# A masked attention layer on one core: scores moved, an eighth home for Q and K, row statistics moved, another set of resident weight sums

## The chip, the cores and the metric

The kernel runs on one core of one Trainium2 chip. The metric is the device time of one execution in microseconds. The core has TensorE (PE, with its weight loads PEld), VectorE (DVE), ScalarE (ACT), GpSimd (POOL) and SyncE (SP), which issues nearly all DMA transfers here.

## What is computed

```python
def layer(x, adj, Wq, bq, Wk, bk, Wv, bv, beta):      # x (128, 128, 768), adj (128, 128, 128), 12 heads of 64
    h = jnp.maximum(_layernorm(x, axis=-1), 0.0)
    q = _split_heads(h @ Wq + bq)
    k = _split_heads(h @ Wk + bk)
    v = _split_heads(h @ Wv + bv)
    scores = jnp.einsum('bhqd,bhkd->bhqk', q, k) / jnp.sqrt(HD)
    adj_e = adj[:, None, :, :]
    scores = jnp.where(adj_e > 0, scores + beta * adj_e, -9000000000000000.0)
    probs = jax.nn.softmax(scores, axis=-1)
    out = jnp.einsum('bhqk,bhkd->bhqd', probs, v)
    return x + out.transpose(0, 2, 1, 3).reshape(B, N, D)
```

All data is float32.

## The kernel before

**Groups and slices.** The 128 batches are worked off in 32 groups of four (`G` from 0 to 31). For each group three products with weights are made, called slices: `qk0` (Q and K of the first six heads), `v` (V of all heads) and `qk1` (Q and K of the last six heads). Group 0 uses plain matrix products (`plain_slice`). In groups 1 to 31 each slice is 15 block products (`product_z`, L525) of a fast matrix multiplication: an activation operand (a block of the transposed normalized rows, `A..`, or a sum of such blocks, `S..`) times a sum of weight blocks (`T`). Each product is 28 matmuls in the profile (L541) and adds to one of four chains a, b, c, d, each of which holds a pair of PSUM banks. The pairs are four in all; score stages and attention take one from the same four.

**Order.** In groups 1 and later nothing is left to a scheduler (`manual_schedule`): `run` (L775) emits a product's matmuls, then the steps listed for its number (`todo`, by `then`), then the masks of scores made before (`masking`), then decodes that are due (`overdue`), then the product's evictions, the trailing ScalarE work, and last the steps listed as "post". Every engine works its instructions off in that order. `ORDER` gives the products' order in a slice. Below, "product n" is the n-th in that order, from 0.

**Weight sums.** The 45 sums T are made once and kept in DRAM, but for those whose places (0 to 44 over the three slices) stand in `RESIDENT` (L114), which stay in SBUF. The others are streamed in every group, 448 KB each, through a ring of five buffers (`load_T`, L325, DMA at L330): when a streamed product has been emitted, the load of the streamed sum five further on is issued on SP's queue.

**Homes and decodes.** A product's result is added out of PSUM into a home, a block of SBUF for one of the six outputs (r, j) of a slice (`home_qk`; additions at L565, first evictions at L555, L556, L559, L561). When an output has all its products, it is decoded on GpSimd (`decode`, L573; L581 to L584 for Q and K, L592 to L596 for V, which goes on into `vring` and frees the home). Homes of Q and K are freed when their scores are emitted. There are six homes, and a seventh in the area `sbig` from group 0's last slice on.

**Scores and attention.** `scores(G, u, j)` (L609, matmuls at L618) needs the two outputs (0, j) and (1, j) of slice `qk`u; it takes a pair, and in the next product VectorE masks and biases it (L626), gives the pair back, and ScalarE takes the exponential (L628). `attend` (matmuls at L671) follows in later products, threaded between their matmuls; `load_xo` (L605) fetches its residual rows. The scores of `qk0` are taken in the `v` slice of the same group. The scores of `qk1` (u = 1) are taken in the `qk0` slice of the next group, at products 1, 3 and after 5.

**Preparation of later groups.** For group G + 2, the rows' mean and variance come from eight half rows (`load_half`, DMA at L404, into three buffers in turn; `half_stats` on VectorE, L412 and L414), in the `v` slice; `row_moments` (L416) turns them into scale and shift (VectorE L420 and L422, GpSimd L424 and L425), which go to DRAM and back by two small transfers (L428, L429) a few products later. `norm` (L439, ScalarE) applies them to x, loaded by `load_x` in four pieces (L189); `to_hT` (L450, VectorE) transposes, and `inner` (L460 to L462, GpSimd) adds the block sums within an `A`. `sum_acts` (L455, VectorE) makes the sums `S..`.

Of the kernel before, what the change touches and what calls it, by code (L numbers as in the profile page):

```python
# [10 lines left out]
F32 = mybir.dt.float32  # L11
# [6 lines left out]
P = 128  # L18
# [12 lines left out]
@with_exitstack  # L31
def kernel(
    ctx: ExitStack,
    tc: tile.TileContext,
    x: bass.AP,
    adj: bass.AP,
    wq: bass.AP,
    bq: bass.AP,
    wk: bass.AP,
    bk: bass.AP,  # L40
    wv: bass.AP,
    bv: bass.AP,
    beta: bass.AP,
    out: bass.AP,
):

    nc = tc.nc
    keep = ctx.enter_context(tc.tile_pool(name="keep", bufs=1))
    bad = keep.tile([1, 1], I32, name="bad")
    args = (x, adj, wq, bq, wk, bk, wv, bv, beta, out)
    direct(tc, *args, bad)
    again = nc.values_load(bad[0:1, 0:1])
    with tc.If(again > 0):
        general(tc, *args)
# [51 lines left out]
LORDER = (1, 4, 0, 8, 5, 2, 10, 3, 6, 7, 13, 9, 11, 12, 14)  # L111
ORDER = {"qk0": ZORDER, "v": ZORDER, "qk1": QORDER}
RING = 5
RESIDENT = (3, 7, 10, 14, 18, 22, 25, 29, 33, 37, 40, 44)  # L114


SPOT = ("S7", "S0", "S5", "S14", "S11", "S6", "S1", "S9", "S10", "S2")
# [8 lines left out]
def direct(ctx, tc, x, adj, wq, bq, wk, bk, wv, bv, beta, out, bad):  # L126
# [14 lines left out]
    NG = B // GRP  # L141
# [10 lines left out]
    const = ctx.enter_context(tc.tile_pool(name="const", bufs=1))  # L152
# [107 lines left out]
    sequence = [(sl, n) for sl in ("qk0", "v", "qk1") for n in ORDER[sl]]  # L260
    resident = {key: const.tile([P, 7, P], F32, name=f"res_{key[0]}_{key[1]}") for key in (sequence[at] for at in RESIDENT)}
    kept, tz = {}, {}
# [55 lines left out]
    def order_of(G, sl):  # L318
        return LORDER if G == NG - 1 and sl == "qk1" else ORDER[sl]
# [184 lines left out]
        while between and next(between[0], None) is None:  # L504
            between.popleft()

    homes = deque(const.tile([P, 7, P], F32, name=f"home{i}") for i in range(6))
    home_of = {}

    def home_qk(G, sl, r, j, zones=False):  # L510
# [264 lines left out]
    def run(products, todo):  # L775
        for at, steps in enumerate(products):
            next(steps)
            behind_product(at, todo)
            next(steps)
            trail()  # L780
            for f in todo.get((at, "post"), ()):
                f()

    def slice_z(G, sl, todo):
        run([product_z(G, sl, n) for n in order_of(G, sl)], todo)
# [163 lines left out]
    def then(at, f, *args):  # L949
        todo.setdefault(at, []).append(lambda: f(*args))  # L950

    def bias(G, *at):
        def go():
            if G not in steps:
                steps[G] = bias_steps(G)
            next(steps[G], None)
        for n in at:
            then(n, go)

    def attention(G, u, at):  # L960
        for n, j in at:
            then(n - 3, load_xo, G, 3 * u + j)
            then((n, "post"), attend, G, 3 * u + j, 5)
# [6 lines left out]
    def turn_act(G, slots):  # L970
        for at, name in slots:
            then(at, to_hT, G, int(name[1]), int(name[2]))
            then(at, inner, G, name)

    def sums_at(G, slots):
        for at, name in slots:
            then(at, sum_acts, G, name)
# [35 lines left out]
    todo.clear()  # L1013
    for n, j in ((1, 0), (2, 1), (3, 2)):
        then((n, "post"), scores, 0, 0, j)
    attention(0, 0, ((11, 2), (13, 1), (15, 0)))
    for n in range(14):
        then(n, step, 2)
    then(1, halve_bias)
    turn_act(1, ((3, "A01"), (4, "A02"), (5, "A00"), (9, "A10"), (10, "A11"), (11, "A12")))  # L1020
    sums_at(1, ((12, "S1"), (13, "S9"), (14, "S10"), (15, "S2")))
    then(12, homes.append, block(len(SPOT)))
    bias(1, 4, 5, 6, 7)
# [4 lines left out]
    for G in range(1, NG):  # L1028
        more = G + 1 < NG
        todo.clear()  # L1030
        then(1, scores, G - 1, 1, 2)
        then(3, scores, G - 1, 1, 0)
        then((5, "post"), scores, G - 1, 1, 1)
        attention(G - 1, 1, ((7, 2), (10, 0), (12, 1)))
        if G == 1:
            sums_at(1, ((0, "S6"), (1, "S7"), (2, "S0"), (5, "S5"), (7, "S14"), (9, "S11")))
            then((0, "post"), load_x, 2, 0)
            for n, at in enumerate((0, 0, 0, 3, 4, 5, 6, 7)):
                then((at, "post"), load_half, 2, n)
            for n, at in enumerate((3, 4, 5, 6, 7, 8, 9, 10)):  # L1040
                then(at, half_stats, 2, n)
            then(10, row_moments, 2, 3, 5)
        else:
            sums_at(G, ((0, "S7"), (1, "S0"), (4, "S5"), (7, "S14"), (9, "S11")))
            if more:
                for g in range(2):
                    for h in range(2):
                        then((2 * g + h, "post"), norm, G + 1, g, 2 * h, 2 * h + 2)
                turn_act(G + 1, ((5, "A01"), (6, "A00"), (11, "A02")))
                then((12, "post"), load_x, G + 1, 1)  # L1050
        slice_z(G, "qk0", todo)

        todo.clear()
        then(0, scores, G, 0, 2)
        then(2, scores, G, 0, 1)
        then(7, scores, G, 0, 0)
        if more:
            then((11, "post"), add_raw, G + 1)
            if G == 1:
                for g in range(2):  # L1060
                    then((2 + g, "post"), norm, 2, g)
                turn_act(2, ((5, "A01"), (6, "A00"), (7, "A02"), (14, "A11")))
                then((8, "post"), load_x, 2, 1)
                for g in range(2, GRP):
                    then((10 + g, "post"), norm, 2, g)
            else:
                for n, at in enumerate((5, 6, 8, 9)):
                    then((at, "post"), norm, G + 1, 2 + n // 2, n % 2 * 2, n % 2 * 2 + 2)
                turn_act(G + 1, ((12, "A11"),))
            if G + 2 < NG:  # L1070
                for n, at in enumerate((0, 0, 0, 3, 5, 6, 8, 9)):
                    then((at, "post"), load_half, G + 2, n)
                for n, at in enumerate((3, 5, 6, 8, 9, 11, 12, 13)):
                    then(at, half_stats, G + 2, n)
        slice_z(G, "v", todo)

        todo.clear()
        if not more:
            break
        attention(G, 0, ((3, 2), (9, 1), (12, 0)))  # L1080
        turn_act(G + 1, ((1, "A10"), (4, "A12")))
        sums_at(G + 1, ((6, "S1"), (7, "S9"), (8, "S2"), (9, "S6"), (10, "S10")))
        bias(G + 1, 0, 2, 4, 5)
        if G + 2 < NG:
            then(5, row_moments, G + 2)
            then((6, "post"), load_x, G + 2, 0)
        slice_z(G, "qk1", todo)

# [150 lines left out]
```

## Time and profile before

| what | value |
|---|---|
| runs | 2904.47, 2900.88, 2901.08 us |
| median | 2901.08 us |
| the profiled execution | 2902.2 us |
| its span, first to last instruction | 2900.4 us |
| mean granted clock of TensorE | 0.97 |
| VectorE, GpSimd, ScalarE busy | 80%, 74%, 52% of the span |
| DMA, main queue | 698.45 MB, 79.2% of 16 engines |

A line of the profile names the source line, the engine, the operation and its tiles (output <- inputs), its shape and how often it stands there; where an engine was idle before it, brackets show for how long and what ended it. Times in the timeline are us from the span's start. One group of the middle runs there from about 1406 (start of `v`) over `qk1` (from 1433) into the next `qk0` (from 1460) and to the next `v` (1495).

### The profile page before, as it was taken

The numbers are of one execution on the slowest core, as the hardware profiler recorded it, in microseconds if no ns is written. First come the engines' busy times: TensorE is split into PE (matmuls) and PEld (weight loads), VectorE is DVE, ScalarE is ACT, GpSimd is POOL, SyncE is SP. The second block draws the span as 40 slices with busy tenths as digits, with TensorE's granted clock in tenths as the row PEclk, the third lists the DMA queues.
The fourth block names the chain that finished last, engine by engine and source line by source line (L and its number), as shares of the span: only waits on it lengthen the run. The fifth ranks groups of instructions, "written<-read, shape, count | busy, mean of one in ns | idle before, by whom it ended". The sixth has DMA issues, their size and how long they took to land.

```text
span 2900.4 us, 121318 instructions
## 1 busy us (share of the span) xinstructions
PE 2753.9 (95%) x52029; PEld 2621.5 (90%) x52029; DVE 2325.4 (80%) x3212; ACT 1497.1 (52%) x3791; POOL 2157.1 (74%) x3170
## 2 busy tenths in 40 slices
PE   9999999999999999999999999999999999999998
PEld 7699998999998989999999999989999999999997
DVE  6897787878888878888878888778887778888775
ACT  1455555555555555555555555555555555555543
POOL 4677777777878777777778787777877787877775
PEclk9999999999999999999999999999999999999999
DMA  8797777978878887788788788787887877888765
GB/s 212 233 282 244 244 229 247 270 246 255 243 233 254 260 249 242 233 253 271 238 249 241 235 256 259 251 237 230 254 271 243 244 242 238 255 259 254 230 212 154
DMA packets 543011, 707.02 MB, mean 244 GB/s; under 512 B 107388, under 2 KB 406152, under 8 KB 542472
## 3 DMA queue, kind: packets, MB, share of 16 engines
q1 hardware_dynamic: 541312, 698.45, 79.2%
q8 instruction: 411, 6.73, 0.9%
q10 hardware_dynamic: 1160, 0.79, 0.1%
q14 instruction: 128, 1.05, 0.1%
HBM read 633.51 MB, written 65.59 MB: 241 GB/s over the span
## 4 chain that ended last, share of the span: by engine, by line
POOL 57%; PE 23%; issue 12%; DVE 4%; ACT 0%; POOLq 0%; DMA 0%; SPq 0%; ACTq 0%; DVEq 0%
PE pair L541 19%; POOL home L584 7%; POOL home L582 6%; POOL home L581 6%; POOL home L583 5%; POOL v L596 5%; POOL home L594 5%; POOL v L595 4%; POOL A L461 3%; POOL home L593 3%; POOL A L460 3%; PE pair L618 3%; POOL v L592 3%; DVE home L565 2%; POOL A L462 2%
## 5 line engine op out<-in xcount | busy, mean ns | idle before, releaser
L565 DVE TENSOR_TENSOR home<-home,pair 128x896 f32<-128x896 f32 x798 | 847.2, 1071 | 235.8 <-PE pair L541 193.4
L541 PE MATMUL pair<-sbig,T_qk 128*64 128x128 f32 x14756 | 961.5, 281 | 7.6 <-DMA T_qk<-kept_qk 4.0
L541 PEld LDWEIGHTS pair<-sbig,T_qk 128*64 128x64 f32 x14756 | 841.4, 142 | 28.3 <-issue 24.5
L654 ACT ACTIVATE e<-e,sm 128x64 f32<-128x64 f32 x1512 | 382.3, 336 | 270.4 <-DVE sm L642 270.3
L541 PE MATMUL pair<-T_v,sbig 128*64 128x128 f32 x7812 | 456.1, 273 | 0.8 <-ACT sbig L556 0.5
L541 PEld LDWEIGHTS pair<-T_v,sbig 128*64 128x64 f32 x7812 | 430.6, 137 | 7.3 <-issue 5.4
L671 PE MATMUL pair<-v,e 128*64 128x65 f32 x6048 | 402.9, 222 | 8.9 <-POOL v L596 8.2
L559 ACT ACTIVATE home<-pair 128x640 f32<-128x640 f32 x319 | 223.5, 700 | 329.5 <-PE pair L541 328.1
L671 PEld LDWEIGHTS pair<-v,e 128*64 128x64 f32 x6048 | 357.8, 137 | 19.9 <-POOL v L596 15.5
L626 DVE SCALAR_TENSOR_TENSOR e<-pair,biasT 128x1024 f32<-128x1024 f32 x189 | 228.0, 1206 | 145.0 <-PE pair L618 141.9
L541 PE MATMUL pair<-A,T_qk 128*64 128x128 f32 x4340 | 333.5, 273 | 0.3 <-DVE home L565 0.2
L460 POOL TENSOR_TENSOR A<-A 128x256 f32<-128x256 f32 x186 | 140.3, 754 | 213.4 <-DVE A L450 213.4
L584 POOL TENSOR_TENSOR home<-home 128x256 f32<-128x256 f32 x319 | 279.5, 876 | 25.0
L618 PE MATMUL pair<-home 64*64 64x128 f32 x5216 | 209.2, 285 | 91.9 <-POOL home L583 85.3
L581 POOL TENSOR_TENSOR home<-home 128x256 f32<-128x256 f32 x319 | 235.6, 739 | 74.0 <-DVE home L565 70.3
L628 ACT ACTIVATE e<-e 128x1024 f32<-128x1024 f32 x189 | 199.9, 1058 | 166.6 <-DVE e L626 166.5
L618 PEld LDWEIGHTS pair<-home 64*64 64x64 f32 x5216 | 144.2, 136 | 141.2 <-POOL home L583 95.0
L541 PE MATMUL pair<-A,res_qk 128*64 128x128 f32 x4340 | 264.3, 273 | 1.0 <-ACT home L561 1.0
L680 ACT COPY e<-pair 128x520 f32<-128x520 f32 x189 | 111.2, 588 | 290.1 <-PE pair L671 289.9
L582 POOL TENSOR_TENSOR home<-home 128x256 f32<-128x256 f32 x319 | 237.0, 743 | 25.0
L541 PEld LDWEIGHTS pair<-A,res_qk 128*64 128x64 f32 x4340 | 240.8, 137 | 1.3 <-ACT home L561 1.3
L439 ACT ACTIVATE x<-x,block 128x192 f32<-128x192 f32 x480 | 234.2, 540 | 3.6 <-DMA x<-in_x_dram 3.6
(186 smaller groups left out, 4656.2 us busy)
## 6 DMA issues: line engine op xcount, KB each, us to landing
T_qk<-kept_qk SPq DMA_DIRECT2D x682, 448.0 KB
T_v<-kept_v SPq DMA_DIRECT2D x341, 448.0 KB
xo<-in_x_dram SPq DMA_DIRECT2D x189, 256.0 KB
out_dram<-xo SPq DMA_DIRECT2D x189, 256.0 KB
x<-in_x_dram SPq DMA_DIRECT2D x248, 192.0 KB
sbig<-in_x_dram SPq DMA_DIRECT2D x186, 192.0 KB
half<-in_x_dram SPq DMA_DIRECT2D x60, 192.0 KB
kept_qk<-prep_qk SPq DMA_DIRECT2D x22, 448.0 KB
```

Of the source, the lines that this page charges most:

```text
L439: nc.scalar.activation(t, t, AF.Relu, bias=shift[G, n], scale=rstd[G, n])
L460: e.tensor_tensor(t[:, 0:2], t[:, 7:8].to_broadcast([P, 2, P]), t[:, 5:7], ALU.subtract)
L541: nc.tensor.matmul(p[q:q + HD, at, :], lhs[:, q:q + HD], rhs, start=(first and at % 4 == 0), stop=True, skip_group_check=True)
L559: nc.scalar.activation(t[:, 0:5], p[:, 0:5], AF.Copy, scale=float(sign))
L565: nc.vector.tensor_tensor(t, t, p[:, 0:7], op)
L581: e.tensor_tensor(t[:, 1:4:2], t[:, 1:4:2], twice(5), ALU.add)
L582: e.tensor_tensor(t[:, 2:5:2], t[:, 2:5:2], twice(1), ALU.add)
L584: e.tensor_tensor(t[:, 0:7:6], t[:, 0:7:6], twice(2), ALU.add)
L618: nc.tensor.matmul(ps[k:k + HD, i, g * N:(g + 1) * N], keys[r, k:k + HD], queries[r], start=True, stop=True)
L626: nc.vector.scalar_tensor_tensor(e, ps, SCORE_CAP * ISCALE, bias, op0=ALU.min, op1=ALU.add)
L654: nc.scalar.activation(o[:, r, b, 0:HD], pa[:, r, b, 0:HD], AF.Copy, scale=t[:, 1, r, b:b + 1])
L671: nc.tensor.matmul(pa[q:q + HD, 2 * g + i, :], k[:, q:q + HD], vt[G, "v", r, h // 4][:, 4 * g + h % 4, :], start=True, stop=True, skip_gro ...
```

## The change

Five places of the schedule change.

- The scores of `qk1` go from products 1, 3 and after 5 of the next `qk0` slice to products 3, 5 and after 6. Group 0's own attention and transpositions of the first slices are shifted by one or two products too.
- There are seven homes to begin with, eight with the one in `sbig`.
- `RESIDENT` has eleven places instead of twelve, nearly all of them others: 34 sums are streamed in each group instead of 33.
- Half rows are loaded from the end of `qk0` on (after products 11, 12 and 13, then after V's products 0 to 4) and their statistics are taken at V's products 0 to 7; `row_moments` goes from `qk1`'s product 5 to V's product 8, and its two small transfers with it.
- The transposition and inner sums of A11 go from V's product 12 to 10.

```diff
-RESIDENT = (3, 7, 10, 14, 18, 22, 25, 29, 33, 37, 40, 44)
+RESIDENT = (3, 8, 12, 16, 20, 25, 29, 33, 35, 38, 41)
...
-    homes = deque(const.tile([P, 7, P], F32, name=f"home{i}") for i in range(6))
+    homes = deque(const.tile([P, 7, P], F32, name=f"home{i}") for i in range(7))
...
-    attention(0, 0, ((11, 2), (13, 1), (15, 0)))
+    attention(0, 0, ((9, 2), (11, 1), (13, 0)))
...
-    turn_act(1, ((3, "A01"), (4, "A02"), (5, "A00"), (9, "A10"), (10, "A11"), (11, "A12")))
+    turn_act(1, ((4, "A01"), (5, "A02"), (6, "A00"), (9, "A10"), (10, "A11"), (11, "A12")))
...
-        then(1, scores, G - 1, 1, 2)
-        then(3, scores, G - 1, 1, 0)
-        then((5, "post"), scores, G - 1, 1, 1)
+        then(3, scores, G - 1, 1, 2)
+        then(5, scores, G - 1, 1, 0)
+        then((6, "post"), scores, G - 1, 1, 1)
...
+        for n, at in enumerate((11, 12, 13) if G + 2 < NG else ()):
+            then((at, "post"), load_half, G + 2, n)
         slice_z(G, "qk0", todo)
...
-                turn_act(G + 1, ((12, "A11"),))
+                turn_act(G + 1, ((10, "A11"),))
             if G + 2 < NG:
-                for n, at in enumerate((0, 0, 0, 3, 5, 6, 8, 9)):
-                    then((at, "post"), load_half, G + 2, n)
-                for n, at in enumerate((3, 5, 6, 8, 9, 11, 12, 13)):
-                    then(at, half_stats, G + 2, n)
+                for n in range(8):
+                    then(n, half_stats, G + 2, n)
+                    if n > 2:
+                        then((n - 3, "post"), load_half, G + 2, n)
+                then(8, row_moments, G + 2)
         slice_z(G, "v", todo)
...
         if G + 2 < NG:
-            then(5, row_moments, G + 2)
             then((6, "post"), load_x, G + 2, 0)
         slice_z(G, "qk1", todo)
```

## What was predicted

> **What bounds the kernel now.** I read the page first, then TensorE's own waits, then one group of four batches on each engine, and last whole groups against each other. The page (columns: busy time, share of the span, instructions):
>
> ```profile
> span 2900.4 us, 121318 instructions
> PE 2753.9 (95%) x52029; PEld 2621.5 (90%) x52029; DVE 2325.4 (80%) x3212; ACT 1497.1 (52%) x3791; POOL 2157.1 (74%) x3170
> ```
>
> TensorE is busy for 95%, so only its gaps and its slow stretches can be won. TensorE's waits (total us, times, longest):
>
> ```profile
> PE pair L618 <- POOL home L583: 85.3, 26, 3.5
> PE pair L618 <- POOL sbig L583: 13.6, 4, 3.4
> PE pair L618 <- POOL home L584: 4.9, 14, 0.4
> PE pair L541 <- DMA T_qk<-kept_qk: 4.0, 1, 4.0
> ```
>
> The first two lines are 30 waits for some 30 groups: one score stage in each group waits up to 3.5 us for the decoding of Q and K on GpSimd. Streamed weight sums (T) made TensorE wait once. Here is that wait in TensorE's timeline, at the start of a QK0 slice:
>
> ```profile
> 1459.57 3.23 PE L541 MATMUL pair<-sbig,T_qk 128*64 128x128 f32 x56
> 1462.73 0.67 PE L618 MATMUL pair<-home 64*64 64x128 f32 x16
> 1466.79 0.45 PE L618 MATMUL pair<-home 64*64 64x128 f32 x8 [3.39 <-POOL home L583]
> 1467.59 0.45 PE L618 MATMUL pair<-home 64*64 64x128 f32 x8 [0.35 <-POOL home L584]
> 1467.97 2.71 PE L541 MATMUL pair<-sbig,T_qk 128*64 128x128 f32 x28
> 1470.46 2.46 PE L541 MATMUL pair<-sbig,res_qk 128*64 128x128 f32 x28
> 1472.85 1.10 PE L618 MATMUL pair<-home 64*64 64x128 f32 x32
> 1473.88 3.28 PE L541 MATMUL pair<-sbig,T_qk 128*64 128x128 f32 x56
> ```
>
> Products 0 and 1 (56 matmuls) take 3.16 us to the next start. A score stage takes 1473.88 - 1472.85 = 1.03 us; this one takes 1467.97 - 1462.73 = 5.24, so 4.21 are lost. And products 2 and 3 then take 1472.85 - 1467.97 = 4.88 instead of some 3.1. The windows (length, busy times of PE, PEld, DVE, ACT, POOL, then clock, DMA share, GB/s) say why, and compare whole groups from score stage to score stage:
>
> ```profile
> 1462.70:1468.00 5.30, 1.55 (x36) 0.87 (x34) 1.43 (x2) 4.04 (x11) 4.99 (x7) 1.00 0.73 210
> 1468.00:1473.00 5.00, 5.00 (x64) 4.83 (x64) 4.21 (x4) 1.93 (x3) 4.61 (x7) 0.66 0.25 66
> 1462.73:1551.03 88.30, 84.24 (x1646) 81.09 (x1644) 72.35 (x97) 47.09 (x121) 67.39 (x99) 0.98 0.82 247
> 2349.80:2438.60 88.80, 85.02 (x1650) 81.57 (x1648) 71.95 (x97) 47.01 (x121) 67.51 (x99) 0.96 0.80 247
> 2616.90:2702.50 85.60, 82.44 (x1649) 79.39 (x1647) 72.81 (x97) 47.54 (x123) 66.67 (x97) 1.00 0.84 253
> ```
>
> After the wait the granted clock is 0.66 for 5 us. The last group kept a clock of 1.00 throughout and lasts 85.60 us rather than 88.3 to 88.8. Its wait was shorter:
>
> ```profile
> 2616.95 0.67 PE L618 MATMUL pair<-home 64*64 64x128 f32 x16
> 2621.30 1.75 PE L541 MATMUL pair<-sbig,T_qk 128*64 128x128 f32 x28
> ```
>
> 4.35 us for the stage, so 3.32 lost; without it that group is 82.28 us. Between the two first starts of this kind (1462.73 and 2616.95) lie 13 groups, 88.8 us each. So the wait with its slow clock costs about 6.5 us in an ordinary group and 3.3 in a rare one; I take 6.1 over 30 groups, for the first groups are shorter: **183 us that can be won**, which would leave 82.3 us a group.
>
> The Trainium skill, page "TensorE: Matmul & The Clock Gate", section Part 1 (the clock gate), says the clock is halved after an idle window of about 3.4 us and that a busy window restores it. The rows agree (3.39 us idle, then 0.66; a shorter idle, then 1.00). Without that rule the sum would be the waits alone, some 104 us less the costs below, which gives 2851 us; with it a shortened wait is worth more than its own length.
>
> **The change part by part.** The stage that waits is the first of the three deferred ones (QK1, pair 2): it needs the fourth of six decodes that GpSimd does one after another. These rows are GpSimd and VectorE in the same group:
>
> ```profile
> 1429.61 0.46 POOL L592 TENSOR_TENSOR v<-home 128x128 f32<-128x128 f32 x1 [3.80 <-DVE home L565]
> 1432.48 0.73 POOL L460 TENSOR_TENSOR A<-A 128x256 f32<-128x256 f32 x1
> 1434.24 0.46 POOL L592 TENSOR_TENSOR v<-home 128x128 f32<-128x128 f32 x1
> 1453.08 1.02 POOL L424 TENSOR_TENSOR row<-verow,nhalf 128x4 f32<-128x4 f32 x1
> 1454.34 0.73 POOL L581 TENSOR_TENSOR home<-home 128x256 f32<-128x256 f32 x1
> 1462.00 1.19 POOL L583 TENSOR_TENSOR home<-home 128x128 f32<-128x128 f32 x1
> 1463.26 1.45 POOL L584 TENSOR_TENSOR home<-home 128x256 f32<-128x256 f32 x1
> 1472.27 1.19 POOL L583 TENSOR_TENSOR sbig<-sbig 128x128 f32<-128x128 f32 x1
> ...
> 1427.44 2.08 DVE L565 TENSOR_TENSOR home<-home,pair 128x896 f32<-128x896 f32 x2 [1.04 <-PE pair L541]
> 1474.02 1.23 DVE L626 SCALAR_TENSOR_TENSOR e<-pair,biasT 128x1024 f32<-128x1024 f32 x1 [0.88 <-PE pair L618]
> 1475.16 0.70 DVE L450 STREAM_TRANSPOSE A<-x 128x512 f32<-128x512 f32 x1
> ```
>
> GpSimd idles until 1429.61 and then shows no gap until the sixth decode ends (1472.27, and one operation more).
>
> *Scores two products later.* The stage moves from product 1 to 3, which is 3.1 us on TensorE: of 4.21 us some 1.1 remain.
>
> *Statistics and A11 earlier.* The inner sums of A11 (1432.48 to 1434.24: 1.76 us) go from V's product 12 to 10, the row moments (1453.08 to 1454.34: 1.26 us) from QK1's product 5 to V's product 8. Both then fall ahead of 1429.61, into GpSimd's idle 3.80 us, and the chain of decodes is shorter by 3.02. VectorE's transposition of A11 (0.70) goes into its idle 1.04 before 1427.44; if the normalizing on ScalarE is late, the eviction behind it and so the chain's start slip by up to 1.3 us (my estimate: one transposition and one short eviction). So the fourth decode comes 1.7 to 3.0 us sooner, against 1.1 needed: **this wait is gone, with 0.6 to 1.9 us to spare**, and with it the slow clock. The second and third stage move by two products and by one: the sixth decode ends at about 1474.2 - 1.7 = 1472.5, and the third stage, undelayed, wants it at about the same time. That is level.
>
> *What is late next: a PSUM pair.* Three chains hold three of the four pairs, so score stages share the fourth. The second and third stage now stand one product apart instead of two and a half. The third can't start before VectorE has masked the second (1.23), behind an eviction (1.04, half of the 2.08) and a transposition (0.70): some 3.0 us after product 5 ends, against 1.03 + 1.5 on TensorE. Cost 0.4 us a group; 0 if the transposition slips behind, 1.5 if the sum for product 4 is late too.
>
> *The eight half rows.* Their loads start three products sooner, and each statistic stands three products behind its load; VectorE takes the eight in V's products 0 to 7 rather than in 3 to 13. If a half is late, VectorE stands still, and behind it wait the masks (which free the pair for the next scores), the evictions, and through them SP's next half load and the T loads in the queue. Rows for it (SP's issues, then VectorE's wait for a half and a mask, then TensorE):
>
> ```profile
> 1408.95 0.99 SPq L404 DMA_DIRECT2D sbig<-in_x_dram  x2
> 1491.36 1.87 SPq L189 DMA_DIRECT2D x<-in_x_dram  x4
> ...
> 1415.41 0.56 DVE L412 BATCH_NORM_STATS2 strow<-sbig 128x6 f32<-128x384 f32 x1 [2.06 <-DMA sbig<-in_x_dram]
> 1497.53 1.23 DVE L626 SCALAR_TENSOR_TENSOR e<-pair,biasT 128x1024 f32<-128x1024 f32 x1
> ...
> 1500.60 1.31 PE L618 MATMUL pair<-home 64*64 64x128 f32 x32
> ```
>
> A half issued at 1408.95 landed at 1415.4: 6.4 us. The second half now stands right behind the four pieces of x, so it is issued at 1493.2 and lands near 1499.6. Its statistic (0.56) stands ahead of the mask that ran at 1497.53; the mask would end at 1501.4, and the scores of 1500.60 wait 0.8 us. Halves 3 to 7 have three products and up to two score stages from issue to need (4.6 + 2.1 us), with the same latency; I put 0.4 on them together. Cost 1.2 us a group; nothing if all land as fast as TensorE allows; above, 3.8 us for one that comes 3.4 late with a slowed clock.
>
> *Homes and weight sums.* With the scores two products later, eight blocks hold Q and K at once, hence the home; it is paid with one resident sum, so 34 sums stream instead of 33. That is 448 KB more a group. DMA works for 0.82 of 88.3 us, 72 us; with 1.4 us more it is 74 of some 84 us. So it isn't the bound on the mean; but the load at the end of QK1 now goes through a narrow place: SP issues four pieces of x at product 6, and behind them the sum for QK1's product 14, which was resident.
>
> ```profile
> 1446.08 2.09 SPq L189 DMA_DIRECT2D x<-in_x_dram  x4
> 1448.28 1.83 SPq L330 DMA_DIRECT2D T_qk<-kept_qk  x2
> ```
>
> The first of these two T loads was for the next product 0, which began at 1459.57, 11.3 us later, without a wait. The sum for product 14 would be issued there and is needed a product (1.5) sooner, 9.8 us later. Cost 0.2 us a group; bounds 0 and 1.5 (one product's lead).
>
> *The rest.* The shifts in group 0 happen once, beside plain products on TensorE: nothing, within one wait of 3.5 us either way. The row moments' two small transfers leave QK1 for V's product 12 and QK1's product 0, past the same SP queue; T loads behind them have their ring of five as cover, at the price of the 0.2 above if it fails. Attention itself keeps its places: scores to probabilities (1.23 on VectorE, then the exponential) has four products now where it had six.
>
> **Sum.** Profiled execution 2902.2 us (the span and 1.8 around it; 1.1 over the median of the runs). Won 183, given back 30 x (0.4 + 1.2 + 0.2) = 54: 129 net, 2773 us; less the 1.1 to the median, **2772 us**.
>
> **The rivals.**
>
> *Nothing is given back.* The halves land in time and the pair is free: 2901 - 183 = 2718. For it: VectorE waits for one half a group now, without a wait of TensorE behind it. Against: the mask's place above. 15%.
>
> *GpSimd is late still.* While the two long operations at 1462.00 and 1463.26 ran, VectorE added two SBUF blocks (S7 and S0); they took 1.19 and 1.45 instead of 0.46 and 0.73. Without the wait VectorE has another such sum (S5) and the residual addition inside the chain of decodes: two more collisions, 1.5 us, more than the 0.6 to spare at the worse end, so a wait of 0.9 to 2 us in each group: 2772 + 27 to 60, 2799 to 2832. 15%. The Trainium skill's page "SBUF — State Buffer", section "Who interferes with whom", has this as a rule: a VectorE operation with two SBUF inputs shuts out a GpSimd operation that reads SBUF. The stretched rows agree.
>
> *The change doesn't take the wait away* (another link of the chain slips as far as the scores): 2895 to 2907. 3%.
>
> *Slower: a half stops V.* If a half lands so late that TensorE stands still for 3.4 us at V's second score stage, the clock drops there as it did in QK0: 6.5 us a group in place of the 6.1 won, and 1.8 of the other costs on top of it: 2901 + 30 x 2.2 = 2967. It decides from a landing at about 1502.2, 9 us after issue where 6.4 was seen. 6%.
>
> **How the numbers follow.** Forecast 2772 with 61%, its own range 2740 to 2798. The range of 8 in 10 takes in both neighbours: 2715 to 2832. Faster by over 0.2% (what a measurement here can tell from no change) is all but the last two rivals: 0.91; within 0.2%: 0.03; slower: 0.06.
>
> **What would show it.** Right: the line of TensorE waiting for L583 falls from 85 us to under 20; the clock stays at 1.00 through QK0's first products; a group lasts about 84 us. The pair: short waits of the third deferred scores for VectorE's mask. The halves: VectorE's wait for half loads grows from one to several a group in V, and scores in V wait for a mask. Wrong: a clock below 1.00 anywhere in a group, or TensorE waiting for T in most groups.

## The result, and the profile after

| kernel | median | runs | ratio to the kernel before, 95% interval |
|---|---|---|---|
| before | 2902.77 us | 2900.88 to 2906.34 | |
| changed | 2861.94 us | 2861.45 to 2869.09 | 0.9864 (0.9845 to 0.9883) |

The change is faster by 1.4%, 41 us. A gain of 129 us was forecast; the time lies above the stated range. The profiled execution of the changed kernel has a span of 2860.4 us and a mean granted clock of 0.995 instead of 0.970.

TensorE's waits in the changed kernel, some lines of the same view as before (total us, times, longest):

```profile
PE pair L618 <- DVE e L626: 44.9, 52, 2.6
PE pair L541 <- DVE home L565: 41.2, 50, 1.7
PE pair L541 <- DVE e L626: 10.7, 20, 1.3
PE pair L541 <- ACT home L556: 8.7, 10, 1.5
...
PE pair L618 <- POOL home L583: 2.5, 1, 2.5
...
PE pair L541 <- DMA T_qk<-kept_qk: 0.3, 1, 0.3
```

The wait for GpSimd's decode, 85.3 and 13.6 us before, is down to 2.5. What was hoped for there has happened. But TensorE now waits for VectorE, at masks (L626) and additions (L565), and for ScalarE at first evictions (L556). No such line stood among the larger ones before. The start of QK0 in TensorE's timeline, to be laid beside the one of before:

```profile
1455.52 0.67 PE L618 MATMUL pair<-home 64*64 64x128 f32 x16
1456.01 0.62 PE L618 MATMUL pair<-sbig 64*64 64x128 f32 x16
1456.56 3.28 PE L541 MATMUL pair<-sbig,T_qk 128*64 128x128 f32 x56
1459.76 1.10 PE L618 MATMUL pair<-home 64*64 64x128 f32 x32
```

The first deferred score stage takes 1456.56 - 1455.52 = 1.04 us instead of 5.24, and two products after it take 3.20 at full clock instead of 4.88. So the place of the loss is elsewhere. Windows show it: the V slice of one group before and of one after, then two whole groups after, an ordinary one and the last but one (columns: length, busy PE, PEld, DVE, ACT, POOL, clock, DMA share, GB/s).

```profile
1406.21:1433.34 27.13, 27.02 (x521) 25.51 (x518) 21.43 (x35) 12.46 (x25) 17.67 (x29) 1.00 0.95 290
```

```profile
1478.94:1509.98 31.04, 27.22 (x521) 25.40 (x518) 23.70 (x39) 12.46 (x25) 19.83 (x33) 1.00 0.90 272
...
1455.52:1542.73 87.21, 82.74 (x1646) 79.33 (x1644) 73.51 (x97) 46.73 (x120) 68.63 (x99) 1.00 0.83 255
2677.86:2761.30 83.44, 82.43 (x1646) 79.36 (x1644) 68.80 (x83) 45.96 (x117) 67.53 (x97) 1.00 0.81 239
```

TensorE's work in V is the same, 27 us, but V lasts 31.04 us instead of 27.13: 3.9 us are lost there. The last row is a group that prepares no rows, since no group G + 2 is left. It takes 83.44 us, 3.8 less. So the trace itself points at the half rows. The clock is 1.00 in the groups shown, but it dropped in V of two others, behind waits of 2.60 and 3.15 us at V's second score stage (the first of them is shown in the last section).

VectorE in that V slice, the rows that matter here:

```profile
1480.83 0.56 DVE L412 BATCH_NORM_STATS2 strow<-sbig 128x6 f32<-128x384 f32 x1
1484.33 0.56 DVE L412 BATCH_NORM_STATS2 strow<-sbig 128x6 f32<-128x384 f32 x1 [1.46 <-DMA sbig<-in_x_dram]
1485.05 1.17 DVE L626 SCALAR_TENSOR_TENSOR e<-pair,biasT 128x1024 f32<-128x1024 f32 x1
1489.93 0.56 DVE L412 BATCH_NORM_STATS2 strow<-sbig 128x6 f32<-128x384 f32 x1 [1.08 <-DMA sbig<-in_x_dram]
1495.25 0.56 DVE L412 BATCH_NORM_STATS2 strow<-sbig 128x6 f32<-128x384 f32 x1 [0.64 <-DMA sbig<-in_x_dram]
1497.57 0.56 DVE L412 BATCH_NORM_STATS2 strow<-sbig 128x6 f32<-128x384 f32 x1 [1.43 <-DMA sbig<-in_x_dram]
1504.13 0.71 DVE L450 STREAM_TRANSPOSE A<-x 128x512 f32<-128x512 f32 x1 [2.20 <-ACT x L439]
1504.77 2.05 DVE L565 TENSOR_TENSOR home<-home,pair 128x896 f32<-128x896 f32 x2
```

Four of the statistics wait for their half. The mask that stood behind the second one ends at 1486.22, and TensorE's next score stage, V's second, which needs its PSUM pair, starts 0.15 us later:

```profile
1486.37 0.67 PE L618 MATMUL pair<-sbig 64*64 64x128 f32 x16 [1.49 <-DVE e L626]
1492.94 1.75 PE L541 MATMUL pair<-T_v,sbig 128*64 128x128 f32 x28 [0.73 <-ACT home L556]
1506.87 1.75 PE L541 MATMUL pair<-T_v,A 128*64 128x128 f32 x28 [1.41 <-DVE home L565]
```

The last row is another matter in part: the addition that TensorE waits for there stood behind the transposition of 1504.13, and that one waited 2.20 us for ScalarE's normalizing (L439).

SP's queue in the same stretch shows why one late half is followed by others:

```profile
1483.43 1.82 SPq L404 DMA_DIRECT2D sbig<-in_x_dram  x2
1487.16 0.33 SPq L404 DMA_DIRECT2D half<-in_x_dram  x1
1490.52 0.33 SPq L404 DMA_DIRECT2D sbig<-in_x_dram  x1
1492.65 0.33 SPq L404 DMA_DIRECT2D sbig<-in_x_dram  x1
```

The eight halves go through three buffers, so SP can issue half n + 3 only when statistic n has been taken. The statistic at 1489.93 ends at 1490.49, and the load for three places further on is issued at 1490.52; it is taken at 1495.25.

### The profile page after: what moved, and what is told of

It is laid out like the page before. It is cut to its first block, busy times and chain, and to the rows that moved or that the text cites. A ratio compares the mean times of both kernels' runs of the same rounds, so it can differ in the third digit from the quotient of the medians.

```text
span 2860.4 us, 121343 instructions
## 1 busy us (share of the span) xinstructions
PE 2699.4 (94%) x52029; PEld 2568.1 (90%) x52029; DVE 2351.8 (82%) x3212; ACT 1489.0 (52%) x3791; POOL 2193.8 (77%) x3170
## 3 DMA queue, kind: packets, MB, share of 16 engines
q14 instruction: 127, 1.04, 0.1%
## 4 chain that ended last, share of the span: by engine, by line
PE 45%; DVE 20%; DMA 15%; ACT 7%; POOL 3%; issue 3%; SPq 2%; ACTq 0%; DVEq 0%; POOLq 0%
PE pair L541 38%; DMA sbig<-in_x_dram 11%; DVE home L565 7%; PE pair L671 4%; DMA x<-in_x_dram 4%; ACT x L439 3%; DVE e L626 3%; PE pair L618 3%; DVE sbig L455 3%; DVE A L450 2%; DVE strow L412 1%; SPq L189 1%; ACT e L628 1%; DVE xo L687 1%; DVE sbig L565 1%
## 5 line engine op out<-in xcount | busy, mean ns | idle before, releaser
L565 DVE TENSOR_TENSOR home<-home,pair 128x896 f32<-128x896 f32 x810 | 856.6, 1071 | 144.6 <-PE pair L541 119.0
L541 PE MATMUL pair<-sbig,T_qk 128*64 128x128 f32 x13888 | 888.2, 274 | 8.6 <-ACT e L680 6.6
L541 PEld LDWEIGHTS pair<-sbig,T_qk 128*64 128x64 f32 x13888 | 754.3, 137 | 27.8 <-issue 11.5
L541 PE MATMUL pair<-A,T_qk 128*64 128x128 f32 x6076 | 416.7, 274 | 9.7 <-DVE home L565 8.1
L541 PE MATMUL pair<-T_v,sbig 128*64 128x128 f32 x6944 | 417.1, 275 | 8.7 <-ACT home L556 7.2
L541 PEld LDWEIGHTS pair<-T_v,sbig 128*64 128x64 f32 x6944 | 385.8, 138 | 20.6 <-ACT home L556 17.6
L559 ACT ACTIVATE home<-pair 128x640 f32<-128x640 f32 x325 | 227.5, 700 | 300.9 <-PE pair L541 269.9
L541 PEld LDWEIGHTS pair<-A,T_qk 128*64 128x64 f32 x6076 | 329.1, 137 | 22.6 <-DVE home L565 14.1
L584 POOL TENSOR_TENSOR home<-home 128x256 f32<-128x256 f32 x325 | 294.9, 907 | 25.5
L582 POOL TENSOR_TENSOR home<-home 128x256 f32<-128x256 f32 x325 | 294.6, 906 | 25.5
L581 POOL TENSOR_TENSOR home<-home 128x256 f32<-128x256 f32 x325 | 243.2, 748 | 62.2 <-DVE home L565 59.3
L460 POOL TENSOR_TENSOR A<-A 128x256 f32<-128x256 f32 x186 | 162.0, 871 | 139.1 <-DVE A L450 139.1
L439 ACT ACTIVATE x<-x,block 128x192 f32<-128x192 f32 x480 | 232.1, 545 | 6.0 <-DMA x<-in_x_dram 6.0
L556 ACT ACTIVATE home<-pair 128x640 f32<-128x640 f32 x160 | 111.9, 699 | 236.3 <-DVE home L555 235.4
L618 PE MATMUL pair<-home 64*64 64x128 f32 x5312 | 189.9, 277 | 46.2 <-DVE e L626 38.8
L626 DVE SCALAR_TENSOR_TENSOR e<-pair,biasT 128x1024 f32<-128x1024 f32 x189 | 226.3, 1197 | 1.5 <-PE pair L618 1.3
L618 PEld LDWEIGHTS pair<-home 64*64 64x64 f32 x5312 | 146.4, 134 | 78.8 <-POOL home L581 20.4
```

The source lines that it names most:

```text
L439: nc.scalar.activation(t, t, AF.Relu, bias=shift[G, n], scale=rstd[G, n])
L541: nc.tensor.matmul(p[q:q + HD, at, :], lhs[:, q:q + HD], rhs, start=(first and at % 4 == 0), stop=True, skip_group_check=True)
L559: nc.scalar.activation(t[:, 0:5], p[:, 0:5], AF.Copy, scale=float(sign))
L565: nc.vector.tensor_tensor(t, t, p[:, 0:7], op)
L581: e.tensor_tensor(t[:, 1:4:2], t[:, 1:4:2], twice(5), ALU.add)
L582: e.tensor_tensor(t[:, 2:5:2], t[:, 2:5:2], twice(1), ALU.add)
```

## The experiments

The theory: a statistic stands ahead of masks and evictions on VectorE and waits for its half row to land; three buffers hand the delay on through V. The rivals: the other resident sums and the extra streamed one, A11 at product 10, or the bare time of the statistics on VectorE. Below, a wait "at product n" is the sum, over all groups, of TensorE's waits of more than 0.05 us ahead of that product. What the expectations call V's third score stage is V's second, the one after product 2.

| kernel | median us | ratio to before, 95% interval | clock |
|---|---|---|---|
| changed | 2861.9 | 0.9864 (0.9845 to 0.9883) | 0.995 |
| statistics back | 2777.4 | 0.9566 (0.9550 to 0.9582) | 0.994 |
| only scores, home, resident sums | 2819.4 | 0.9719 (0.9699 to 0.9740) | 0.993 |
| masks first | 2831.5 | 0.9758 (0.9736 to 0.9780) | 0.995 |
| A11 back | 2884.5 | 0.9942 (0.9921 to 0.9964) | 0.994 |
| statistics back, A11 at 11 | 2845.0 | 0.9798 (0.9781 to 0.9814) | 0.991 |
| three halves loaded | 2802.1 | 0.9645 (0.9621 to 0.9669) | 0.993 |
| statistics alone, on the kernel before | 2965.2 | 1.0225 (1.0206 to 1.0243) | 0.971 |
| statistics back, old resident sums | 2779.9 | 0.9583 (0.9567 to 0.9599) | 0.996 |
| three halves, second ahead of x | 2780.3 | 0.9570 (0.9554 to 0.9586) | 0.996 |
| second half ahead of x | 2851.5 | 0.9811 (0.9791 to 0.9831) | 0.992 |
| statistics back, normalizing early | 2749.1 | 0.9471 (0.9455 to 0.9487) | 0.996 |
| the same, third scores later | 2762.7 | 0.9515 (0.9499 to 0.9530) | 0.996 |

**Statistics back.** One part of the change is undone:

```diff
-        for n, at in enumerate((11, 12, 13) if G + 2 < NG else ()):
-            then((at, "post"), load_half, G + 2, n)
...
-                for n in range(8):
-                    then(n, half_stats, G + 2, n)
-                    if n > 2:
-                        then((n - 3, "post"), load_half, G + 2, n)
-                then(8, row_moments, G + 2)
+                for n, at in enumerate((0, 0, 0, 3, 5, 6, 8, 9)):
+                    then((at, "post"), load_half, G + 2, n)
+                for n, at in enumerate((3, 5, 6, 8, 9, 11, 12, 13)):
+                    then(at, half_stats, G + 2, n)
...
+            then(5, row_moments, G + 2)
```

> The changed kernel with the half-row loads, their statistics and the row moments where they were before the change (loads after V's products 0, 0, 0, 3, 5, 6, 8, 9; statistics at 3 to 13; moments at QK1's product 5). Theory A (the halves hold VectorE up in V, and through its masks and evictions TensorE): TensorE's waits in V for masks and first evictions (44.6 us ahead of V's third score matmuls, 10.8 at product 10, 8.2 at product 6) go, a group takes about 84 us instead of 87, and the time is 2765 to 2800 us, though the moments are back in GpSimd's chain. Theory B (the other resident sums, the extra streamed sum or A11 at product 10 make the loss): within 20 us of the changed kernel's 2862.

2777.4 us, 85 less than the changed kernel. TensorE's waits and a group:

```profile
PE pair L541 <- DVE home L565: 26.6, 51, 0.8
PE pair L618 <- DVE e L626: 10.6, 30, 2.6
```

```profile
1418.00:1501.90 83.90, 82.58 (x1646) 79.25 (x1645) 72.69 (x97) 46.69 (x121) 68.43 (x98) 1.00 0.88 265
```

A group lasts 83.9 us instead of 87.2. None of its score stages (L618) waits for L583, although the row moments are in GpSimd's chain again. So the moved statistics cost the 85 us, and their move wasn't needed for the scores. Theory A holds. The 10.6 us for masks, 0.35 a group, stand at the third deferred scores. 12.6 us are left at V's product 13.

**Only scores, home and resident sums.** As above, and A11 is at product 12 too: `turn_act(G + 1, ((12, "A11"),))`.

> The kernel before with only the later scores, the eighth home and the other resident sums; halves, statistics, moments and A11 as before the change. Theory A: two products are 3.1 of the 4.2 us that the first deferred score stage lost, so some 1.1 us of wait for GpSimd stays in each group, too short to slow the clock; 0.4 for the PSUM pair; 2755 to 2800 us, and no wait of TensorE for a mask in V. Theory B (the moved GpSimd work is what removes the wait, and without it the wait slips along and the clock still drops): above 2850 us, granted clock under 0.985.

2819.4 us: outside the ranges of both theories, nearer to A's. The clock stays up but in four groups, and more is left of the wait than 1.1 us a group:

```profile
PE pair L618 <- POOL home L583: 35.2, 23, 1.7
PE pair L618 <- DVE e L626: 11.0, 30, 2.6
PE pair L618 <- POOL home L584: 9.2, 24, 1.1
PE pair L671 <- POOL v L596: 7.7, 25, 0.4
PE pair L618 <- POOL sbig L583: 7.6, 5, 1.7
```

The three lines of score stages are 52 us, 1.7 a group. So two products later, with the home that this needs, is worth 84 us, and A11 two products earlier, the only difference to the experiment before, is worth 42 more.

**Masks first.** The changed kernel with the order turned round within a product:

```diff
-        for f in todo.get(at, ()):
-            f()
         for f in pending:
             f()
+        for f in todo.get(at, ()):
+            f()
```

> The changed kernel with one thing altered: in each product the pending masks are emitted ahead of the listed steps, so on VectorE a mask stands before the half statistic of that product and not behind it. Theory A: TensorE's wait for masks ahead of V's third score stage (44.6 us) and at product 10 (10.8 us) go; first evictions still wait behind late halves; 30 to 55 us less than the changed kernel. Theory B (VectorE is late in V by the sum of its work, or TensorE waits for something that only coincides): less than 10 us of difference, the waits turn up at the evictions.

2831.5 us, 30 less than the changed kernel: the lower edge of A. The wait ahead of V's second score stage falls from 44.6 us to 5.1, but at product 10 it grows from 10.8 to 25.9. So the place of a statistic ahead of a mask is part of the loss. What is left stands mainly at product 13 (39.9 us, 38.8 before this edit), where TensorE waits for VectorE's addition, and at product 10.

**A11 back.** The changed kernel with `turn_act(G + 1, ((12, "A11"),))`.

> The changed kernel with A11's transposition and inner sums back at V's product 12. Theory A1 (at product 10 the transposition waits for ScalarE's normalizing, 2.2 us in the group looked at, and holds up the eviction that product 13 waits for): the wait at V's product 13 (38.8 us) goes to under 10 us and the time falls by 20 to 40 us, unless GpSimd's chain, 1.8 us longer, makes the deferred scores wait again. Theory A2 (VectorE is late there because of the halves before it): the wait stays over 25 us and the time changes by less than 10 us.

2884.5 us, 23 more than the changed kernel. The wait at product 13 goes, as A1 had it, but the deferred scores wait for GpSimd again, which A1 named only as an exception. TensorE's waits:

```profile
PE pair L618 <- DVE e L626: 40.1, 47, 3.0
PE pair L618 <- POOL home L584: 30.3, 28, 3.1
```

**Statistics back, A11 at 11.** The first experiment with `turn_act(G + 1, ((11, "A11"),))`.

> The first experiment's kernel (statistics and moments back where they were, 2777 us) with A11's transposition and inner sums at V's product 11 instead of 10. There TensorE waited 12.6 us ahead of V's product 13, behind the transposition that waits for ScalarE's normalizing (87.9 us of VectorE's time). Theory A: a product later the normalizing is done; the 12.6 us go, GpSimd's chain has the room, 2760 to 2772 us. Theory B: the chain of decodes starts later by as much, and the deferred scores at QK0's products 3 and 5 wait again: 2780 to 2800 us.

2845.0 us, 68 more than with product 10: B in kind, and dearer than its range. TensorE waits for GpSimd's decodes as with product 12:

```profile
PE pair L618 <- POOL home L583: 38.0, 23, 1.7
PE pair L671 <- POOL v L595: 16.2, 29, 0.7
```

At product 10 the inner sums fit into GpSimd's idle time; at 11 they stand in the way of the decode that starts the chain. It is also 26 us dearer than product 12 (2819.4 us): attention in QK1 waits longer for V's decodes (16.2 us against 7.7), and the clock drops in eight groups against four. Whether that is all of the 26 is open.

**Three halves loaded.** The changed kernel, with the halves 3 to 7 left unloaded from group 3 on (lines in the trace are 3 higher):

```diff
+        if n > 2 and G > 2:
+            rows[G, g, h] = left_rows[n % 3]
+            return
...
-        rows[G, g, h] = t
+        rows[G, g, h] = left_rows[n % 3] = t
```

> The changed kernel, statistics at V's products 0 to 7 and moments at 8 as there, but from group 3 on only the first three half rows are loaded, and the other five statistics read those three again (five of eight loads are left out, so the rows' means and variances are taken from other rows). VectorE's instructions are all there, in the same places. Theory A (a statistic stands ahead of the masks and evictions and waits for its half to land): TensorE's waits at V's third score stage and after go nearly all, 2765 to 2800 us. Theory B (the statistics' own time on VectorE in early V, 5 us a group, is too much there, wherever the halves are): above 2835 us.

2802.1 us, 60 less than the changed kernel with all of VectorE's instructions in place, at the edge of A. The wait at product 13 falls from 38.8 us to 9.6. What stays in V is the wait ahead of its second score stage, 44.4 us; 33.2 of them are in the first line here, whose other 10.9 are the third deferred scores:

```profile
PE pair L621 <- DVE e L629: 44.1, 48, 3.8
PE pair L544 <- DVE home L568: 16.3, 50, 0.3
```

**Statistics alone.** The kernel before with the statistics, loads and moments of the change, and nothing else of it.

> The kernel before with only the half rows, statistics and moments moved as in the change; scores at products 1, 3 and after 5, seven homes, the old resident sums, A11 at product 12. Theory A: V loses some 3 us a group to late halves, and the deferred scores still wait for GpSimd and the clock still drops, for VectorE's lag at V's end delays the chain as much as the moved moments relieve it: 2940 to 3000 us. Theory B: the lost time in V is taken out of the wait for GpSimd, which goes on regardless of TensorE: 2870 to 2905 us.

2965.2 us, 2.2% slower than the kernel before: A. Both waits stand side by side:

```profile
PE pair L618 <- POOL home L583: 79.6, 29, 2.8
PE pair L618 <- DVE e L626: 49.0, 23, 3.4
```

**Statistics back, old resident sums.** The first experiment with `RESIDENT = (3, 7, 10, 14, 18, 22, 25, 29, 33, 37, 40)`.

> The first experiment's kernel (2777 us) with the resident sums of before, less the last one (place 44, which had to go for the home). Theory A: which sums are resident makes no difference that counts, since TensorE hardly ever waits for a streamed one (4.0 us before, 0.3 after): within 8 us of the first experiment. Theory B: the old set leaves six streamed products in a row behind the loads of x at the end of QK1, and TensorE waits for T there by 0.5 to 1.5 us in each group: 15 to 45 us more.

2779.9 us against 2777.4, intervals that overlap: which sums stay resident makes no difference that could be measured.

**Three halves, the second ahead of x.** The kernel of three halves with loads after QK0's products 11, 11 and 13 instead of 11, 12 and 13.

> The kernel of three half rows (five of eight loads left out, their statistics read the first three again; 2802 us), with the second half loaded after QK0's product 11, ahead of the four pieces of x, and not after 12, behind them. Theory A (what is left there, 44.4 us ahead of V's third score stage, is the second half landing behind x): the wait goes to under 10 us, 2755 to 2772 us. Theory B (it is another lag of VectorE that the mask meets at this place): within 10 us of 2802.

2780.3 us: 22 less than without, between the two theories. The wait at V's second score stage falls from 44.4 us to 5.7. VectorE now waits for the third half instead (53.4 us in 28 waits), which costs TensorE less: 10.9 us ahead of product 6. It stays 82 us below the changed kernel, in which these eight statistics stand at the same places. So it is the landing of the halves, and not the statistics' own time.

**The second half ahead of x.** The changed kernel with that one load moved, all halves loaded.

> The changed kernel with that one load moved: the second half after QK0's product 11 instead of 12. Theory A (each late half costs by itself): the 44.6 us ahead of V's third score stage go, the waits at products 6, 10 and 13 stay, 2810 to 2835 us. Theory B (the late halves of a chain make up for one another: when one comes in time, VectorE waits for the next by as much, since they follow each other through three buffers): less than 15 us gained, 2847 or more.

2851.5 us, 10 less: B. V's second score stage hardly waits (3.3 us), and product 6 waits 46.6 us instead of 8.2:

```profile
DVE strow L412 <- DMA half<-in_x_dram: 51.7, 36, 2.5
...
PE pair L541 <- ACT home L556: 42.8, 25, 3.5
PE pair L541 <- DVE home L565: 35.4, 53, 1.4
...
PE pair L618 <- DVE e L626: 12.4, 32, 2.8
```

The first line is VectorE waiting for the buffer of the third and sixth half, 6.3 us in 12 waits before this edit. When one half comes in time, the next one is the late one.

**Normalizing early.** The first experiment with one line changed:

```diff
-                for n, at in enumerate((5, 6, 8, 9)):
+                for n, at in enumerate((4, 5, 6, 7)):
```

> The first experiment's kernel (2777 us) with the four steps of normalizing that A11 needs after V's products 4, 5, 6 and 7 instead of 5, 6, 8 and 9. Theory A (A11's transposition at product 10 waits for them on VectorE, 87.9 us in all, and TensorE pays 12.6 us of it at product 13): the 12.6 us go, 2760 to 2770 us. Theory B (VectorE or ScalarE meets the load of x or another eviction instead): within 5 us, or slower.

2749.1 us, better than both kernels by far and more than expected. The wait at V's product 13 is gone, and VectorE's wait for normalizing falls from 87.9 us to 37.1. So A11 at product 10 cost 28 us as long as the normalizing stayed where it was. A group:

```profile
1401.10:1484.00 82.90, 82.12 (x1646) 79.39 (x1644) 72.88 (x97) 46.78 (x121) 68.96 (x98) 1.00 0.89 270
```

82.9 us, 0.6 above the 82.3 that the prediction had worked out for a group without loss.

**The third scores later.** On top of it, `then(7, scores, G - 1, 1, 1)` and the first attention after product 8.

> The kernel with normalizing early, and the third deferred scores at QK0's product 7 instead of after 6, the first deferred attention after product 8 instead of 7. Theory A (the third score stage waits for the PSUM pair that the second one's mask gives back, 10.6 us): that wait goes, 8 to 12 us less than with normalizing early alone. Theory B (attention then waits for its probabilities, or GpSimd's sixth decode was what bound it): within 4 us.

2762.7 us, 14 more: neither theory. The wait for the pair goes, but another for a pair comes at product 10, where attention, a product later, hasn't been copied out (23.1 of these 28.4 us):

```profile
PE pair L541 <- ACT e L680: 28.4, 32, 5.3
```

## Why the prediction was wrong, step by step

*What bounds the kernel* was right. The wait for GpSimd and the slow clock behind it were worth nearly what was said: with them gone and nothing else in the way, a group takes 82.9 us (normalizing early), where 82.3 were worked out.

*Scores two products later* was right in kind. It took the clock's drop away in all but four groups, and alone it left 1.7 us a group where some 1.1 was forecast.

*Statistics and A11 earlier*: the 1.76 us of A11 were needed and are worth 42 us. The 1.26 us of the row moments were not: with them back in the chain the scores didn't wait. A second step failed here. The slip behind late normalizing was bounded at 1.3 us, but counted against GpSimd's chain alone; that TensorE's product 13 waits for the addition behind it was put at nothing. It cost 28 us, 0.9 a group, measured without the moved statistics (normalizing early).

*The PSUM pair*: 0.4 us a group forecast, 0.35 measured in the first experiment.

*Homes and weight sums*: 0.2 us a group forecast; TensorE waited for a streamed sum once, 0.3 us in all. The 34th streamed sum was not taken back by itself in any run; it is in the kernel of 2749 us too.

*The eight half rows* is the step that failed most, as a size: 1.2 us a group forecast, 2.8 measured (85 us over 30 groups, statistics back). The 3.9 us that the shown V slice lost hold the normalizing behind A11 as well. The mechanism was the one described, down to the mask and the pair at V's second score stage (0.8 forecast, 1.49 in the group shown). The mistake was to price the later halves as if each were issued at its place in the list, with 6.7 us to its need. The change had also cut the lead of halves 3 to 7, from four or five products between load and statistic to three. SP can issue a half only when the statistic three places before is taken, so a late one makes the next one late. The 0.4 us put on halves 3 to 7 were 2.0 (60 us, when they aren't loaded). Half of that stands ahead of product 13, where TensorE waited 38.8 us in all after the change and 9.6 without those loads: with VectorE's first additions late, ScalarE's eviction and normalizing are late, and A11's transposition at product 10 waits for them.

With the measured sizes the sum comes near: 183 - 30 x 0.4 - 85 - 28 = 58 us won, where 41 were measured. Of the 17 that are left, 9.7 stand ahead of QK1's product 13, where TensorE hardly waited before (0.2); why it does now stays open. Without the moved statistics the kernel takes 2777 us; that this is close to the 2772 forecast with them is chance. The time lies above the range because its worse end was set by one rival (GpSimd still late) and not by the upper bound of the half rows, 3.8 us a group, which stood in the text and would have given 2850. That bound counted on a slowed clock in V, as did the rival of a half that stops V; it came in two groups only.

## What to carry to other kernels

On an engine that works in order, an instruction that waits for a transfer belongs behind the evictions and masks that others wait for, or far enough behind its load that it seldom waits; moving both load and use forward together gains no lead. Where transfers go round few buffers, price the whole loop of load, use and next load, not each load from its place in the list. And when a change has several parts, the trace may hold the experiment already: here the last group but one, which prepares no rows, took 3.8 us less.

## What the runs showed of the hardware that was not expected

The clock dropped after shorter gaps than 3.4 us, and not after every gap of one length. Two gaps in the kernel with the statistics alone, each with the window behind it:

```profile
1225.51 1.51 PE L618 MATMUL pair<-home 64*64 64x128 f32 x16 [2.83 <-POOL home L583]
1228.00:1233.00 5.00, 5.00 (x66) 4.83 (x66) 3.06 (x4) 2.18 (x4) 4.68 (x6) 0.60 0.29 94
...
534.10 1.10 PE L618 MATMUL pair<-home 64*64 64x128 f32 x32 [2.81 <-DVE e L626]
534.10:539.10 5.00, 5.00 (x104) 4.83 (x106) 4.96 (x9) 1.93 (x3) 3.27 (x5) 1.00 0.92 325
```

After 2.83 us without a matmul the clock was 0.60, while a gap of 2.81 us left it at 1.00. It also dropped after 2.60 us in the changed kernel, and after 1.69 us (with another 0.35 behind a few matmuls) in the one with A11 at 11:

```profile
1223.71 0.67 PE L618 MATMUL pair<-home 64*64 64x128 f32 x16 [2.60 <-DVE e L626]
1223.71:1228.71 5.00, 5.00 (x74) 4.67 (x76) 4.84 (x8) 1.65 (x2) 3.42 (x5) 0.66 0.91 324
...
1445.68 0.45 PE L618 MATMUL pair<-sbig 64*64 64x128 f32 x8 [1.69 <-POOL sbig L583]
1445.70:1450.70 5.00, 4.65 (x56) 4.24 (x58) 1.84 (x2) 2.53 (x8) 4.68 (x7) 0.67 0.11 34
```

The Trainium skill's page "TensorE: Matmul & The Clock Gate", Part 1, names an idle window of about 3.4 us that runs free of the kernel. The rows don't agree with a need for a full 3.4 us without matmuls, and they show no sharp edge below it. In all traces of this case together, their starts and ends left out, a slow clock followed within 3.5 us on each of the 30 gaps of more than 3.2 us, 48 of the 81 between 1.9 and 3.2, and 12 of the 87 between 1.5 and 1.9. Whether the place of a gap in such a window, or a few matmuls at its ends, decides it wasn't tried.
